# Between two graph layers: four chunks in turn on ScalarE, and the attention weights loaded in that stretch

## The chip, the cores and the metric

The kernel runs on one core of a Trainium2 chip. The metric is the device time of one execution in microseconds (us); lower is better. Times of whole executions are medians of several runs; all times inside the execution come from one profiled execution, counted in us from the start of its span.

## The reference

There are 3125 nodes with 256 features and 50000 edges sorted by target. Two layers follow one another; each adds a graph convolution and an attention to `x`, then a mixture of experts. Around the change, the reference computes:

```python
x = x + L0_ffn(layernorm(x))            # 8 experts, 2 per node: two rows per node come back
xn = layernorm(x)
x = x + L1_gnn(xn, edges) + L1_mix(xn)
# L1_gnn: per node 2 x (64 features, 4 attention scores) = xn @ W; per edge a softmax-weighted
#         sum, over the edges of a target, of the source's row
# L1_mix: q, k, v = xn @ Wqkv.T; dots = k_normed.T @ v_normed; out = q @ dots / n @ Wout.T + bout
```

## The kernel before

`x` stays in SBUF as 125 partitions x 25 tiles x 256, and is worked through in seven chunks of tiles (`CHUNKS`: four of 4 tiles, three of 3).

The **stretch between the layers** is `experts_in` (line 1357). Layer 0's experts have scattered two rows for each node into `y2` in HBM. `experts_in` issues the loads of all seven chunks at once, as tiles `y_in`; the first half of each chunk goes on SyncE's queue (SP), the second half on ScalarE's own queue (ACT). The helper `move` (line 63) splits each load into one DMA of 112 and one of 13 partitions, so there are 14 DMAs on each of the two queues. Then, chunk by chunk:

- `moments` (line 1372): VectorE adds both halves into `x`, takes mean and variance (`bn_stats`, `bn_aggr`), and ScalarE takes the square root.
- `table` (line 1382): VectorE takes the reciprocal and the negative mean (lines 1385 and 1386); ScalarE normalises each tile (`ln_row`, line 1390); TensorE transposes into `ln_pt` (line 1395); ScalarE copies the transposed rows to `xT` (line 1396); TensorE multiplies each tile by `wcat` into a PSUM tile `pw` (line 191), and ScalarE copies each of these 136 columns wide results into `t1_st` (line 1401). SP stores the chunk to the table `tab1` in HBM.

The order is written out by hand for TensorE, VectorE, ScalarE and SP: `moments` of chunk c, then the whole of `table` of chunk c-1. So all of ScalarE's steps for one chunk stand one after another, with TensorE's steps between them.

The **edge loop** follows in `layer1_mix` (lines 1307 to 1332). For 49 groups of 8 edge columns, GpSimd gathers 8 x 128 rows of `tab1` by indirect DMA (`fetch`, line 1212, four buffers `g1`; 391 gathers in all), VectorE makes messages (`messages`, line 1219, line 1223 the first instruction), and TensorE sums them into targets (`products`). A gather can read any row of `tab1`, so the first one waits for the last store. In between, `galerkin` (line 1501) does the attention in steps (`next(todo)`). Before its first `yield` it loads four weight tiles `nat4` to `nat4d` (512 KB each) and `bout` on SP (lines 1512 and 155), transposes three of the tiles into `wkv` and `woT` (lines 1520 to 1528), adds `bout` to all chunks of `x` on VectorE (line 1533) and takes the mean of each head out of `wkv` (lines 1536 to 1538). Only then come the first messages.

The tiles of the loop lie in pools that reuse the memory of `experts_in`; `late` (line 1196, GpSimd), `top` (line 1204) and `dots` (line 1530) are the first instructions to touch it. In the loop and its preparation TensorE, VectorE and ScalarE follow the written order; SP and GpSimd are placed by the framework's planner. Layer 1's expert stage (`layer1_ffn`) begins when the loop and its tail are done.

Of the kernel before, what the change touches and what calls it, by code (L numbers as in the profile page):

```python
# [8 lines left out]
F32 = mybir.dt.float32  # L9
# [9 lines left out]
D = 256  # L19
P = 125  # L20
NT = 25
CHUNKS = ((0, 4), (4, 4), (8, 4), (12, 4), (16, 3), (19, 3), (22, 3))
# [40 lines left out]
def move(queue, out, in_):  # L63


    for s in (slice(0, 112), slice(112, P)):
        queue.dma_start(out[s], in_[s])  # L67
# [7 lines left out]
def rows_of(table):  # L75
    return table.rearrange("(t p) d -> p t d", p=P)
# [12 lines left out]
class Kernel:  # L89
# [1082 lines left out]
    def layer1_mix(self):  # L1172
        nc, tc, a = self.nc, self.tc, self.a
        W, HD = 68, 64
        with ExitStack() as m:
            E_ = mybir.EngineType
            xp = m.enter_context(tc.tile_pool(name="l1x", bufs=1))
            xT = xp.tile([128, 2, N], F32, name="xT2")
            tab1 = self.tab1 = self.dram.tile([N, 2 * W], F32, name="tab1")
            with tc.tile_pool(name="l1l", bufs=1) as lp, \  # L1180
                    tc.tile_pool(name="l1lp", bufs=3, space=PSUM) as pl, \
                    tc.tile_pool(name="l1lm", bufs=4, space=PSUM) as pm, \
                    tc.manual_schedule(engines={E_.PE, E_.DVE, E_.Activation, E_.SP}):
                self.experts_in(lp, pl, pm, xT)
            big = m.enter_context(tc.tile_pool(name="l1", bufs=1))
            wk = m.enter_context(tc.tile_pool(name="l1w", bufs=2))
            gp = m.enter_context(tc.tile_pool(name="l1g", bufs=3))
            ps_a = m.enter_context(tc.tile_pool(name="l1pa", bufs=2, space=PSUM))
            ps_c = m.enter_context(tc.tile_pool(name="l1pc", bufs=1, space=PSUM))
# [22 lines left out]
            def fetch(j0):  # L1212
                n = min(GROUP, NJ - j0)
                g = gp.tile([128, GROUP, 2 * W], F32, name="g1", bufs=4)
                for i in range(n):
                    gather(nc, g[:, i, :], tab1[:], self.t_src[:, j0 + i:j0 + i + 1])
                return j0, n, g
# [61 lines left out]
            def weigh(n, o, v):  # L1279
                nc.vector.tensor_mul(v[:, :n, :, :HD], o[:, :n, None, :HD].to_broadcast([128, n, 4, HD]),  # L1280
                                     v[:, :n, :, HD:].to_broadcast([128, n, 4, HD]))
# [23 lines left out]


            with tc.manual_schedule(engines={E_.PE, E_.DVE, E_.Activation}):
                todo = self.galerkin(big, wk, ps_a, ps_c, xT)
                next(todo)
                starts = [(j0, min(GROUP, NJ - j0)) for j0 in range(0, NJ, GROUP)]  # L1310
                G = len(starts)
                ahead = [fetch(starts[i][0]) for i in range(3)]
                msg, exps, summed = {}, {}, {}
                for i in range(G + 2):
                    if i + 3 < G:
                        ahead.append(fetch(starts[i + 3][0]))
                    if i < G:
                        j0, n, g = ahead[i]
                        o, s, pt = messages(j0, n, g)
                    next(todo, None)  # L1320
                    if 0 <= i - 1 < G:
                        weigh(starts[i - 1][1], msg[i - 1][0], exps[i - 1][2])
                    if i < G:
                        pb = maximum(pt)
                    if 0 <= i - 1 < G:
                        summed[i - 1] = products(*starts[i - 1], exps[i - 1][2], msg[i - 1][1])
                    if 0 <= i - 2 < G:
                        add(*starts[i - 2], *exps[i - 2][:2], summed[i - 2])
                    if i < G:
                        msg[i] = o, ones_of(j0, n)  # L1330
                        exps[i] = exponents(n, s, pb)
                    next(todo, None)
                last = exps[G - 1][0]
# [6 lines left out]
            keep = big.tile([128, 1], F32, name="keep")  # L1340
# [7 lines left out]
            for t0, n in CHUNKS:  # L1348
                s = slice(t0, t0 + n)
                for t in range(t0, t0 + n):  # L1350
                    for h in range(4):
                        xs = self.x[:, t, h * HD:(h + 1) * HD]
# [1 line left out]
                                                       op0=OP.mult, op1=OP.add)  # L1354
        self.layer1_any_order()

    def experts_in(self, pool, psum, psum_m, xT):

        nc, W = self.nc, 68
        mv = pool.tile([P, NT, 2], F32, name="ln_mv2")
        rs = pool.tile([P, 2, NT], F32, name="ln_rs2")
        y2 = self.y2[:2 * N].rearrange("(i t p) d -> p i t d", i=2, p=P)
        loads = []
        for t0, n in CHUNKS:
            r = pool.tile([P, 2, 4, D], F32, name="y_in", bufs=len(CHUNKS))
            for i, queue in enumerate((nc.sync, nc.scalar)):
                move(queue, r[:, i, :n, :], y2[:, i, t0:t0 + n, :])
            loads.append(r)  # L1370

        def moments(r, t0, n):
            s = slice(t0, t0 + n)
            for i in range(2):
                nc.vector.tensor_add(self.x[:, s, :], self.x[:, s, :], r[:, i, :n, :])
            st = pool.tile([P, 4, 6], F32, name="ln_st2", bufs=2)
            for t in range(t0, t0 + n):
                nc.vector.bn_stats(st[:, t - t0, :], self.x[:, t, :])
                nc.vector.bn_aggr(mv[:, t, :], st[:, t - t0, :])
            nc.scalar.activation(rs[:, 0, s], mv[:, s, 1], AF.Sqrt, bias=self.eps[:P])  # L1380

        def table(t0, n):
            s = slice(t0, t0 + n)

            nc.vector.reciprocal(rs[:, 0, s], rs[:, 0, s])
            nc.vector.scalar_tensor_tensor(rs[:, 1, s], mv[:, s, 0], -1.0, rs[:, 0, s], op0=OP.mult, op1=OP.mult)
            row = pool.tile([P, 4, D], F32, name="ln_row2", bufs=2)
            for i in range(n):
                t = t0 + i
                nc.scalar.activation(row[:, i, :], self.x[:, t, :], AF.Identity, bias=rs[:, 1, t:t + 1],  # L1390
                                     scale=rs[:, 0, t:t + 1])
            for k in range(2):
                pt = psum.tile([128, 4, P], F32, name="ln_pt")
                for i in range(n):
                    nc.tensor.transpose(pt[:, i, :], row[:, i, k * 128:(k + 1) * 128], self.ident[:P, :P])
                nc.scalar.copy(xT[:, k, t0 * P:(t0 + n) * P], pt[:, :n, :].rearrange("p a b -> p (a b)"))
            st = pool.tile([P, 4, 2 * W], F32, name="t1_st", bufs=2)
            for i in range(n):
                pm = psum_m.tile([P, 4, 65], F32, name="pw").rearrange("p h c -> p (h c)")[:, :2 * W]
                self.token_matmul(pm, xT, t0 + i, self.wcat)  # L1400
                nc.scalar.copy(st[:, i, :], pm)
            move(nc.sync, rows_of(self.tab1)[:, t0:t0 + n, :], st[:, :n, :])

        before = None
        for r, chunk in zip(loads, CHUNKS):
            moments(r, *chunk)
            if before is not None:
                table(*before)
            before = chunk
        table(*before)  # L1410

    def layer1_any_order(self):

# [84 lines left out]
                nc.vector.tensor_mul(o, o, den[:, :n, :, None].to_broadcast([P, n, 4, HD]))  # L1498
                nc.vector.tensor_add(self.x[:, s, :], self.x[:, s, :], acc[:, :n, 4:])

    def galerkin(self, big, wk, ps_a, ps_c, xT):

        nc, a = self.nc, self.a
        nats = []
        for name, src in (("nat4", a["L1_mix_Wqkv"][512:1024, :].rearrange("(c p) d -> p c d", p=128)),
                          ("nat4b", a["L1_mix_Wqkv"][1024:1536, :].rearrange("(c p) d -> p c d", p=128)),
                          ("nat4c", a["L1_mix_Wout"].rearrange("(c p) f -> p c f", p=128)),
                          ("nat4d", a["L1_mix_Wqkv"][0:512, :].rearrange("(c p) d -> p c d", p=128))):  # L1510
            nat = wk.tile([128, 2, 512] if name == "nat4c" else [128, 4, D], F32, name=name, bufs=1)
            nc.sync.dma_start(nat, src)
            nats.append(nat)
        bout = self.bcast(big, "L1_mix_bout")
        wkv = big.tile([128, 2, 1024], F32, name="wkv")
        for c4 in range(2):
            for k in range(2):
# [10 lines left out]
            nc.scalar.copy(woT[:, :, cc * 128:(cc + 1) * 128], pt)  # L1528
        dots = big.tile([128, 4, 128], F32, name="dots")
        nc.vector.memset(dots, 0.0)  # L1530
        for t0, n in CHUNKS:
            xs = self.x[:, t0:t0 + n, :]
            nc.vector.tensor_add(xs, xs, bout[:, None, :].to_broadcast([P, n, D]))
        heads = wkv.rearrange("p k (h c) -> p (k h) c", c=64)
        mean = big.tile([128, 32], F32, name="wkv_mean")
        nc.vector.tensor_reduce(mean, heads, AX.X, OP.add)
# [40 lines left out]
        for i in range(2):  # L1577
            pm = ps_a.tile([128, 2, D], F32, name="ln_pt")
# [8 lines left out]
        pm = ps_a.tile([128, 2, D], F32, name="ln_pt")  # L1587
# [7 lines left out]
        for t0 in range(0, NT, 2):  # L1595
            m = min(2, NT - t0)
            pm = ps_a.tile([P, 2, D], F32, name="ln_pt")
# [3 lines left out]
            xs = self.x[:, t0:t0 + m, :]  # L1601
# [397 lines left out]
```

## Time and profile before

| what | value |
|---|---|
| median of 3 runs | 3148.76 us (3139.96 to 3158.86) |
| the profiled execution's own time | 2766.24 us |
| its span | 2764.5 us |
| mean granted TensorE clock in it | 0.884 |
| stretch: last instruction of layer 0's experts on GpSimd to first gather | 1535.39 to 1612.23 us |
| first messages of the edge loop | 1634.98 us |
| last gather of the edge loop | 2189.54 us |

The profile tells for every engine what ran when, and for each idle stretch which event ended it. The profiled execution is 382 us shorter than the median of the timed runs, and nothing shown says in which stages those lie.

### The profile page before, as it was taken

How to read it: one execution, taken by the hardware profiler on the slowest of the kernel's cores; microseconds unless marked ns; L12 is line 12 of the kernel's file. 1: busy time of each engine (PE TensorE's matmuls, PEld its weight loads, DVE VectorE, ACT ScalarE, POOL GpSimd, SP SyncE). 2: the span in 40 equal slices, each digit the busy share in tenths (PEclk: the TensorE clock that was granted, in tenths of full speed). 3: DMA queues.
4: the chain of work that ended last, by engine and by line, in shares of the span. 5: the costliest groups of instructions: out<-in, count | busy, mean ns of one | idle time of the engine just before them, and what ended most of it. 6: DMA issues, size and time to landing. Idle time of an engine off the chain costs nothing. (4 is left out here: it accounts for less than half of the span.)

```text
span 2764.5 us, 26618 instructions
## 1 busy us (share of the span) xinstructions
PE 2192.9 (79%) x9047; PEld 1649.0 (60%) x9047; DVE 1502.0 (54%) x3575; ACT 545.3 (20%) x1115; POOL 1660.4 (60%) x1486
## 2 busy tenths in 40 slices
PE   1762659999976997899999459998777756999953
PEld 1541447866754665788888336665655544666643
DVE  7986499455477901122112449998777760222226
ACT  2420000000011111222222234444000021223313
POOL 4888787774000813666666158778777507777751
PEclk9955669999986999999999669999898868999976
DMA  8930534133400303455554421111111121112252
GB/s 296 382 111 14 118 76 107 43 72 91 115 32 2 87 19 130 157 179 180 191 196 139 113 76 47 48 48 45 47 48 49 37 68 39 26 40 60 54 105 71
DMA packets 175937, 259.79 MB, mean 94 GB/s; under 512 B 53839, under 2 KB 140857, under 8 KB 172402
## 3 DMA queue, kind: packets, MB, share of 16 engines
q1 hardware_dynamic: 114273, 198.43, 23.2%
q0 software_dynamic: 52288, 47.17, 7.3%
q10 hardware_dynamic: 9222, 12.30, 1.5%
q8 instruction: 76, 1.25, 0.2%
q14 instruction: 78, 0.64, 0.1%
HBM read 173.99 MB, written 83.69 MB: 93 GB/s over the span
## 5 line engine op out<-in xcount | busy, mean ns | idle before, releaser
L58 POOL DMA_INDIRECT adj<-ch_sum,ch_place x391 | 506.3, 1295 | 150.4 <-issue 111.6
L51 POOL DMA_INDIRECT g<-tab,t_src x391 | 459.6, 1175 | 119.7 <-issue 106.8
L58 POOL DMA_INDIRECT sorted<-s_rows,pos x256 | 245.1, 958 | 183.5 <-DVE s_rows L1059 114.0
L460 PE MATMUL psum<-sup,adjT 125*125 125x256 f32 x1250 | 294.4, 395 | 51.0 <-DMA adjT<-adj 40.3
L1288 PE MATMUL pw<-v,hot 128*125 128x260 f32 x1244 | 306.9, 407 | 0.0
L51 POOL DMA_INDIRECT G<-tabg,g_src x256 | 253.7, 991 | 80.2 <-issue 71.5
L460 PEld LDWEIGHTS psum<-sup,adjT 125*125 125x125 f32 x1250 | 242.1, 195 | 92.9 <-DMA adjT<-adj 42.5
L1288 PEld LDWEIGHTS pw<-v,hot 128*125 128x125 f32 x1244 | 244.4, 200 | 43.6
L866 PE MATMUL ph<-xs,w 128*128 128x256 f32 x960 | 219.1, 387 | 23.1 <-issue 20.1
L866 PEld LDWEIGHTS ph<-xs,w 128*128 128x128 f32 x960 | 183.3, 193 | 58.0 <-issue 33.4
L894 PE MATMUL py<-w,h 128*128 128x256 f32 x960 | 216.7, 379 | 0.0
L1715 PE MATMUL fpy<-fw,fh 128*125 128x256 f32 x800 | 184.9, 387 | 33.6 <-DVE y L1717 28.3
L894 PEld LDWEIGHTS py<-w,h 128*128 128x128 f32 x960 | 180.1, 190 | 23.3
L1715 PEld LDWEIGHTS fpy<-fw,fh 128*125 128x125 f32 x800 | 151.5, 191 | 71.1 <-DVE y L1717 29.9
L868 ACT ACTIVATE h<-ph,b 128x256 f32<-128x256 f32 x240 | 113.7, 474 | 361.1 <-PE ph L866 329.3
L1707 PE MATMUL fph<-xT,fw 128*128 128x500 f32 (+1 forms) x448 | 175.5, 541 | 0.2 <-DMA fw<-in_L_ffn_W_dram 0.2
L1034 PE MATMUL pctx<-s_mv,s_ro 128*128 128x256 f32 x512 | 155.5, 415 | 1.9 <-DVE s_mv L1033 1.9
L58 POOL DMA_INDIRECT slots<-rows,abi x50 | 72.7, 1455 | 100.8 <-DVE r_cum L948 85.8
L897 DVE TENSOR_SCALAR yo<-py,own 128x256 f32<-128x256 f32 x60 | 27.8, 481 | 190.8 <-PE py L894 190.8
L1709 ACT ACTIVATE fh<-fph,cols 128x500 f32<-128x500 f32 (+1 forms) x112 | 70.3, 633 | 295.6 <-PE fph L1707 262.5
L463 DVE TENSOR_TENSOR x<-x,psum 125x512 f32<-125x512 f32 (+1 forms) x104 | 68.7, 663 | 109.6 <-PE psum L460 109.5
L1707 PEld LDWEIGHTS fph<-xT,fw 128*128 128x128 f32 x448 | 84.8, 190 | 71.4 <-issue 48.6
(537 smaller groups left out, 3352.8 us busy)
## 6 DMA issues: line engine op xcount, KB each, us to landing
adjT<-adj SPq DMA_DIRECT2D x25, 1367.2 KB
adj<-zero SPq DMA_DIRECT2D x22, 1536.0 KB
w<-in_L_ffn_W1p_dram SPq DMA_DIRECT2D x30, 1024.0 KB
w<-in_L_ffn_W2p_dram SPq DMA_DIRECT2D x30, 1024.0 KB
slots<-empty SPq DMA_DIRECT2D x1, 8448.0 KB
srow<-slots SPq DMA_DIRECT2D x30, 264.0 KB
adj<-ch_sum,ch_place POOLq DMA_INDIRECT x391
g<-tab,t_src POOLq DMA_INDIRECT x391
```

Source lines behind the costliest of these rows:

```text
L51: nc.gpsimd.indirect_dma_start(out=out, out_offset=None, in_=table, in_offset=bass.IndirectOffsetOnAxis(ap=idx, axis=0))
L58: return nc.gpsimd.indirect_dma_start(out=table, out_offset=bass.IndirectOffsetOnAxis(ap=idx, axis=0), in_=rows, in_offset=None, **kw)
L460: nc.tensor.matmul(pm[:, i, :], mats[b][:, (a0 + i) * P:(a0 + i + 1) * P], sup[:, b, :], start=(b == b0), stop=(b == b0 + n - 1))
L463: nc.vector.tensor_add(xs, xs, pm[:, :m, :])
L866: nc.tensor.matmul(ph, w1[:, k, f * 128:(f + 1) * 128], xs[:, k, :], start=(k == 0), stop=(k == 1))
L868: nc.scalar.activation(h[:, f, :], ph, AF.Gelu, bias=b1[:, f:f + 1])
L894: nc.tensor.matmul(py, h[:, f, i * 128:(i + 1) * 128], w2[:, f, :], start=(f == 0), stop=(f == FC - 1))
L1034: nc.tensor.matmul(p1, ro[:, f - f0, :], mv, **st)
L1288: nc.tensor.matmul(pw.rearrange("p h c -> p (h c)"), hot[:, i - i0, :], v[:, i, :, :].rearrange("p h c -> p (h c)"), start=(i == i0), stop ...
L1707: nc.tensor.matmul(ph[:, :n * P], w1[:, k, f * 128:(f + 1) * 128], xT[:, k, t0 * P:(t0 + n) * P], start=(k == 0), stop=(k == 1))
L1709: nc.scalar.activation(hs[:, f, :n * P], ph[:, :n * P], AF.Gelu, bias=self.col("L1_ffn_b1", ei * FC + f))
L1715: nc.tensor.matmul(py, hs[:, f, i * P:(i + 1) * P], w2[:, f, :], start=(f == 0), stop=(f == FC - 1))
```

## The change

It has three parts.

1. The loads. Both halves of every `y_in` chunk are issued on SP; ScalarE issues none. Behind them on SP, still in `experts_in`, come the four attention weight tiles and `bout` (`attention_weights`). These tiles now live in the pool `l1x` beside `xT`.
2. The order. `table` is cut into `rows` (reciprocal, negative mean and normalising), `turned` (transposes and copies to `xT`) and `table` (multiplication, copies, store). One turn of the loop takes `moments` of chunk c, `rows` of c-1, `turned` of c-2 and `table` of c-3. Two tiles' results share one PSUM tile and are copied by one instruction, so 25 copies become 14; `t1_st` has three buffers, where it had two.
3. The bias. The seven additions of `bout` to `x` stand at the end of `experts_in`, ahead of the edge loop's stage, and no longer in `galerkin`.

```diff
         for t0, n in CHUNKS:
             r = pool.tile([P, 2, 4, D], F32, name="y_in", bufs=len(CHUNKS))
-            for i, queue in enumerate((nc.sync, nc.scalar)):
-                move(queue, r[:, i, :n, :], y2[:, i, t0:t0 + n, :])
+            for i in range(2):
+                move(nc.sync, r[:, i, :n, :], y2[:, i, t0:t0 + n, :])
             loads.append(r)
+        nats, bout = self.attention_weights(keep)
...
-        def table(t0, n):
+        def rows(t0, n):
...
+            return row
+
+        def turned(row, t0, n):
             for k in range(2):
...
                 nc.scalar.copy(xT[:, k, t0 * P:(t0 + n) * P], pt[:, :n, :].rearrange("p a b -> p (a b)"))
-            st = pool.tile([P, 4, 2 * W], F32, name="t1_st", bufs=2)
-            for i in range(n):
-                pm = psum_m.tile([P, 4, 65], F32, name="pw").rearrange("p h c -> p (h c)")[:, :2 * W]
-                self.token_matmul(pm, xT, t0 + i, self.wcat)
-                nc.scalar.copy(st[:, i, :], pm)
+
+        def table(t0, n):
+            st = pool.tile([P, 4, 2 * W], F32, name="t1_st", bufs=3)
+            for i in range(0, n, 2):
+                m = min(2, n - i)
+                pm = psum_m.tile([P, 2, 256], F32, name="pw")[:, :, :2 * W]
+                for j in range(m):
+                    self.token_matmul(pm[:, j, :], xT, t0 + i + j, self.wcat)
+                nc.scalar.copy(st[:, i:i + m, :], pm[:, :m, :])
             move(nc.sync, rows_of(self.tab1)[:, t0:t0 + n, :], st[:, :n, :])
...
-        before = None
-        for r, chunk in zip(loads, CHUNKS):
-            moments(r, *chunk)
-            if before is not None:
-                table(*before)
-            before = chunk
-        table(*before)
+        ready = {}
+        for c in range(len(CHUNKS) + 3):
+            if c < len(CHUNKS):
+                moments(loads[c], *CHUNKS[c])
+            if 0 <= c - 1 < len(CHUNKS):
+                ready[c - 1] = rows(*CHUNKS[c - 1])
+            if 0 <= c - 2 < len(CHUNKS):
+                turned(ready.pop(c - 2), *CHUNKS[c - 2])
+            if 0 <= c - 3 < len(CHUNKS):
+                table(*CHUNKS[c - 3])
+        for t0, n in CHUNKS:
+            xs = self.x[:, t0:t0 + n, :]
+            nc.vector.tensor_add(xs, xs, bout[:, None, :].to_broadcast([P, n, D]))
+        return nats
```

`attention_weights` holds the loads that stood at the head of `galerkin`, unchanged but for the pool:

```diff
+    def attention_weights(self, pool):
...
+            nat = pool.tile([128, 2, 512] if name == "nat4c" else [128, 4, D], F32, name=name, bufs=1)
+            nc.sync.dma_start(nat, src)
+            nats.append(nat)
+        bout = self.bcast(pool, "L1_mix_bout")
+        return nats, bout
```

More of the change, by code (lines that the diff above doesn't have):

```diff
@@ L1183, in layer1_mix @@
                     tc.manual_schedule(engines={E_.PE, E_.DVE, E_.Activation, E_.SP}):
-                self.experts_in(lp, pl, pm, xT)
+                nats = self.experts_in(lp, xp, pl, pm, xT)
             big = m.enter_context(tc.tile_pool(name="l1", bufs=1))
@@ L1307, in layer1_mix @@
             with tc.manual_schedule(engines={E_.PE, E_.DVE, E_.Activation}):
-                todo = self.galerkin(big, wk, ps_a, ps_c, xT)
+                todo = self.galerkin(big, wk, ps_a, ps_c, xT, nats)
                 next(todo)
@@ L1355, in layer1_mix, with experts_in @@
         self.layer1_any_order()
-    def experts_in(self, pool, psum, psum_m, xT):
+    def attention_weights(self, pool):
+        nc, a = self.nc, self.a
+        nats = []
+        for name, src in (("nat4", a["L1_mix_Wqkv"][512:1024, :].rearrange("(c p) d -> p c d", p=128)),
+                          ("nat4b", a["L1_mix_Wqkv"][1024:1536, :].rearrange("(c p) d -> p c d", p=128)),
+                          ("nat4c", a["L1_mix_Wout"].rearrange("(c p) f -> p c f", p=128)),
+                          ("nat4d", a["L1_mix_Wqkv"][0:512, :].rearrange("(c p) d -> p c d", p=128))):
+            nat = pool.tile([128, 2, 512] if name == "nat4c" else [128, 4, D], F32, name=name, bufs=1)
[3 more added lines that the diff above has]
+        return nats, bout
+    def experts_in(self, pool, keep, psum, psum_m, xT):
         nc, W = self.nc, 68
@@ L1499, in layer1_any_order, with galerkin @@
                 nc.vector.tensor_add(self.x[:, s, :], self.x[:, s, :], acc[:, :n, 4:])
-    def galerkin(self, big, wk, ps_a, ps_c, xT):
+    def galerkin(self, big, wk, ps_a, ps_c, xT, nats):
         nc, a = self.nc, self.a
[L1506 to L1514, printed above, removed]
         wkv = big.tile([128, 2, 1024], F32, name="wkv")
@@ L1530, in galerkin @@
         nc.vector.memset(dots, 0.0)
-        for t0, n in CHUNKS:
-            xs = self.x[:, t0:t0 + n, :]
-            nc.vector.tensor_add(xs, xs, bout[:, None, :].to_broadcast([P, n, D]))
         heads = wkv.rearrange("p k (h c) -> p (k h) c", c=64)
```

## The prediction

> **What bounds the kernel now.** The page's first part gives no engine more than 79% of the span, so I read the stretch that is edited and then what follows it. First the waits between 1536 and 1640 us, longest first (engine, line, what it waited for, us, times, longest):
>
> ```profile
> POOL late L1196 <- DMA tab<-t_st: 74.8, 1, 74.8
> ACT L1380 <- DMA y_in<-y: 40.3, 1, 40.3
> ...
> DVE ln_rs L1385 <- ACT ln_rs L1380: 21.6, 5, 9.5
> DVE top L1204 <- DMA tab<-t_st: 12.5, 1, 12.5
> DVE x L1533 <- SPq L1418: 11.3, 1, 11.3
> ```
>
> GpSimd does nothing for 74.8 us, until the last table store lands. VectorE loses 21.6 us to square roots. The "SPq L1418" of the last line had long been done; what that addition still lacked is its load, `bout`. Then ScalarE's and GpSimd's timelines:
>
> ```profile
> 1538.36 24.10 ACTq L67 DMA_DIRECT2D y_in<-y  x14
> 1562.48 1.28 ACT L1380 ACT_TABLE_LOAD   x1 [40.33 <-DMA y_in<-y]
> 1563.78 0.49 ACT L1380 ACTIVATE ln_rs<-ln_mv,eps 125x4 f32<-125x4 f32 x2
> ...
> 1611.16 0.10 POOL L1196 MEMSET late<- 128x1 f32 x1 [74.81 <-DMA tab<-t_st]
> 1612.23 0.98 POOL L51 DMA_INDIRECT g<-tab,t_src  x1 [0.96 <-POOL late L1196]
> ```
>
> ScalarE spends 24.10 us issuing 14 DMAs (each 0.31 us; it is held up between them[...]), and takes the first root at 1563.8, though VectorE had the moments at 1549.97. From 1562.48 to its last copy (1608.54) it is the pace: a chunk of four costs 7.1 us (roots at 1572.08, 1579.16, 1586.26), in which it waits for TensorE (12.7 us in all before the copies of `pw`). Store and landing take it to the first gather, 1612.23.
>
> Who paces the edge loop? In the waits of 1660 to 2190 us, VectorE's and GpSimd's longest:
>
> ```profile
> DVE msg L1223 <- DMA g<-tab,t_src: 66.1, 44, 3.4
> POOL g L51 <- issue: 97.8, 321, 0.3
> POOL g L51 <- DMA g<-tab,t_src: 5.2, 17, 0.3
> ```
>
> In 44 of some 46 groups the messages wait for the gather, and GpSimd waits for nobody (0.3 us of issue between gathers). So GpSimd, gather after gather, carries the end: the loop's end moves with the **first gather**, not with the first messages (1634.98).
>
> **What the Trainium skill says.** *DMA: Bandwidth & Descriptors*, "Issuing engines are not separate DMA queues": DMAs of several engines run on the same 16 DMA engines, and a second issuer saves only issue time. The trace agrees and more: in tenths of a microsecond from 1537, SP alone and then both queues,
>
> ```profile
> GB/s 287 369 246 0 0 0 0 0 0 0 0 0 0 0 0 0 0 0 0 0 0 113 154 82 72 0 0 61 164 184 297 317 358 399 379 369 369 379 399 338
> ```
>
> SP alone reaches 369 to 399 GB/s; with both, 1540 to 1565 has a mean of 240. *SBUF — State Buffer*, "Who interferes with whom": a VectorE instruction with two SBUF inputs contends with a GpSimd one that reads SBUF. The trace agrees: while `bout` is added, four gathers take 1.54, 1.97, 1.70 and 1.43 us, not 0.94. *TensorE: Matmul & The Clock Gate*, "What's actually happening": the clock is halved when idle and released by activity; the granted clock here is 0.50 until 1570 and 0.84 in 1570 to 1575.
>
> **Part by part.** *Loads.* ScalarE loses its 24.1 us of issuing. SP issues 28 loads, then 5. At 370 GB/s the 6.4 MB take 17 us from 1539.1, at 240 they take 27. The first chunk, 1.02 MB, lands near 1543 by the former (2.8 us plus about 1.2 to signal, as now), at 1545.2 as now by the latter. The 2.2 MB of weights follow, another 6 to 9 us: all issued by about 1565 to 1572. Queued behind them on SP are the table stores; the first comes at about 1563 to 1568 and can wait a few us; only the last, 20 us later, is waited for. I take 1543.
>
> *Pace.* With ScalarE free VectorE sets it. Its chunk of four takes 4.92 us (1564.40 to 1569.32), that of three 3.68 plus 0.25 for the two small ones. From 1543.0: `moments` end at 1547.7, 1552.4, 1557.3, 1562.2, 1566.1, 1570.1 and **1574.0**. A landing is late only if its chunk misses these starts; at 240 GB/s none does by over 2.2 us. ScalarE needs per turn a root (0.3), four normalisings (2.06), two copies (1.16) and two of 272 columns. Those the trace does not show: copies of 136, 375 and 500 columns take 0.27, 0.475 and 0.58, so 0.39 by interpolation; *ScalarE: Activation LUTs*, "What ACT_TABLE_LOAD costs", gives 186 ns + 0.833 per element, 0.41. I take 0.39. Sum 4.3 us, under 4.92. TensorE's turn takes about 3.7 us at full clock (8 transposes 1.3, 16 multiplications 2.4), 6.7 at half: if it stays slow it adds up to 2 us a turn. VectorE no longer waits for roots: each is a turn old.
>
> *Tail.* The price of the depth: after 1574.0 ScalarE still has, in order, rows 5 (1.57), turned 4 (0.86), table 3 (0.78), rows 6 (1.57), turned 5 (0.86), table 4 (0.66), turned 6 (0.86), table 5 (0.66), then table 6 behind its multiplications (1.8 us at full clock, 3.0 at half) and 0.66: 10.3 to 11.5 with the multiplications, about 1 more for handovers. Last copy about 1586. Store, landing, `late` and first gather take 3.7 as now (1608.54 to 1612.23): **first gather near 1590, 22 us earlier**.
>
> *Bias.* The seven additions (7.24 us) run from about 1574.5 to 1583, the last after rows 6 has read `x`; cover: ScalarE's tail, to 1586. Uncovered they delay only `wkv`'s mean. Out of the gathers' time they give GpSimd back 0.60 + 1.03 + 0.76 + 0.49 = **2.9 us**, unless other work slides in there; then 0.
>
> *Weights.* On landing by 1572 at the latest they cost nothing: transposes and copies (1614.90 to 1621.98, part of it waiting) become about 5 us from 1587, and the mean (4.8 us) ends by 1600. The first group has 8 gathers at 1.25 plus about 2 to land: 1602. First messages move 33 us, from 1635 to 1602, but 10 of these are no gain in a loop that follows GpSimd.
>
> Larger tiles in `l1x`: 17 KB more per partition. They shift the others; nothing in the trace prices that. Bounds: gain 2 us, loss 5; taken 0.
>
> Sum: 22 + 3 = 25 us of 2766.24, **2741** in the profile. The timed runs are 382 us longer and the trace does not show where. As a lump outside, 25 remains 25 and gives 3124; spread evenly, 25 x 3148.76 / 2766.24 = 28.5. I take the latter: **3120**. About 0.5%, 16 us, is what a measurement of this kernel tells from no change.
>
> **Rivals.** *B: the messages count.* If in timed runs TensorE or VectorE paces the loop (TensorE is 92% busy in 1700 to 1800 us at clock 1.00; a lower clock would fill it), the loop moves with its first messages: 33 us, up to 37 scaled, 3112 to 3116. Against: the 44 waits.
>
> *C: the stretch gives less.* Loads at 150 GB/s bring the last chunk at 1582 and the first gather to 1602; or TensorE at half clock adds 2 us in four turns. Gain 10 to 17 with the bias: 3132 to 3139. For: a single queue with 1 KB rows was seen alone for under 2 us here; against: the weights came at 303 GB/s on SP alone (1612 to 1615).
>
> *D, slower: one queue starves the stretch.* The first gather comes about 20 us after the last landing (3.7 + 12 + 3.7). Even with before, counting the 2.9, means a last landing at 1595: 6.4 MB in 56 us, **114 GB/s**; below that rate it loses. At 85 GB/s, landing 1614 and first gather 1634: 19 us lost, about 3168 to 3170. Against: every rate above.
>
> *E: it doesn't do what it says,* since one queue's stop holds all: no more than C.
>
> **How the numbers follow.** Chances: forecast 0.63 (gain 18 to 34), B 0.12, C and E 0.19, D 0.06. The low end is B with some spread, 3106; the high end most of C, 3137. Faster by over 0.5%: 0.61 + 0.12 + 0.08 = 0.81; within: 0.13, C's smaller gains and 0.02 of spread; slower: 0.06.
>
> **What would show it.** Right: ScalarE's first root near 1549; last `moments` near 1574; first gather 1586 to 1594; first messages 12 us later, not 23; gathers of that time at 0.94 us; 44 waits of the messages as before. Wrong: VectorE waiting for `y_in` in mid stretch (C, D); waits of ScalarE for TensorE in every turn (C); a first gather 20 us earlier, with a last one that is not (the loop's pace is not GpSimd's); another length after the loop.

## The result, and the profile after

| what | before | after |
|---|---|---|
| median of the timed runs | 3148.94 us (14 runs) | 3124.68 us (14 runs) |
| ratio, with its 95% interval | | 0.9919 [0.9896, 0.9941], some 25.5 us less |
| span of the profiled execution | 2764.5 us | 3119.1 us |
| mean granted TensorE clock in it | 0.884 | 0.843 |

The forecast was 3120 (3106 to 3137), faster. Two of the 14 executions before fell in a slower state (3205 and 3209 us) and are left out of the ratio, which is therefore not the quotient of the two medians.

The two profiled executions are of different length, so their spans can't be subtracted. I read both from one mark, the start of the last scatter of `y` by GpSimd (1535.4 before, 1788.0 after), and cut the difference of 354.6 us at the loop's last gather: **+252.6** before the mark, **-24.2** from the mark to the last gather (654.15, now 629.96), **+126.1** behind it. The first and the last part come from the length of the execution and not from the change: three variants of the changed kernel that were profiled in short executions (`e9`, `e10`, `e11`, below) reach the mark at 1529.7 to 1535.1 and need 573.6 to 577.4 us behind the last gather; the kernel before, 1535.4 and 575.0. So the gain is in the edited stretch:

| us after the last scatter of `y` | before | after |
|---|---|---|
| `y_in` loads issued until | 27.1 | 26.3 |
| first and last square root | 28.4, 62.6 | 14.6, 39.1 |
| last copy into `t_st` starts | 72.9 | 47.6 |
| additions of `bout` | 87.7 to 94.0 | 39.7 to 46.0 (starts) |
| **first gather** | **76.8** | **51.5** |
| first messages | 99.6 | 64.3 |
| last gather | 654.1 | 630.0 |
| from first to last gather | 577.3 | 578.4 |

First, the waits of the stretch (1785 to 1900 us; engine, line, what it waited for, us in all, times, longest):

```profile
POOL late L1196 <- SPq L1447: 49.8, 1, 49.8
ACT L1394 <- DMA y_in<-y: 26.5, 1, 26.5
...
DVE x L1389 <- DMA y_in<-y: 8.6, 2, 8.1
...
ACT ln_rs L1394 <- DVE ln_mv L1393: 7.5, 4, 2.9
...
ACT t_st L1422 <- PE pw L191: 0.7, 1, 0.7
```

GpSimd's wait is 25.0 us shorter (it was 74.8; the event named is SP's next one behind the table stores). ScalarE's waits have turned round: it used to be late for VectorE (21.6 us of VectorE's waits for a root), now ScalarE waits for VectorE's moments. Before the copies out of `pw` it waits 0.7 us, where the kernel before had

```profile
ACT t_st L1401 <- PE pw L191: 12.7, 25, 0.9
```

VectorE waits for `y_in` only at the start. ScalarE's timeline (start, us, form, and in brackets the idle time before it) shows the start and the tail:

```profile
1801.29 1.28 ACT L1394 ACT_TABLE_LOAD   x1 [26.50 <-DMA y_in<-y]
1802.59 0.30 ACT L1394 ACTIVATE ln_rs<-ln_mv,eps 125x4 f32<-125x4 f32 x1
1805.74 0.30 ACT L1394 ACTIVATE ln_rs<-ln_mv,eps 125x4 f32<-125x4 f32 x1 [2.86 <-DVE ln_mv L1393]
...
1815.58 0.30 ACT L1394 ACTIVATE ln_rs<-ln_mv,eps 125x4 f32<-125x4 f32 x1 [1.65 <-DVE ln_mv L1393]
...
1818.80 0.67 ACT L1422 COPY t_st<-pw 125x272 f32<-125x272 f32 x2
...
1833.78 0.69 ACT L1422 COPY t_st<-pw 125x272 f32<-125x272 f32 x2
1835.17 0.69 ACT L1422 COPY t_st<-pw 125x272 f32<-125x272 f32 x2 [0.70 <-PE pw L191]
```

The roots come 4.9 us apart (1805.74, 1810.66, 1815.58), VectorE's pace and no longer ScalarE's 7.1, and two 272-column copies, one right behind the other, take 0.67 together. GpSimd's and VectorE's timelines show what follows:

```profile
1838.79 0.10 POOL L1196 MEMSET late<- 128x1 f32 x1 [49.80 <-SPq L1447]
1839.57 0.98 POOL L51 DMA_INDIRECT g<-tab,t_src  x1 [0.68 <-POOL late L1196]
```
```profile
1827.77 7.23 DVE L1438 TENSOR_TENSOR x<-x,b_L_mix_bout 125x1024 f32<-125x1024 f32 x7
...
1852.37 0.72 DVE L1223 TENSOR_TENSOR msg<-g,t_dir 128x544 f32<-128x544 f32 x1 [6.55 <-DMA g<-tab,t_src]
```

The seven additions lie beside ScalarE's tail. The first messages wait for gathers, 12.8 us after the first of them; before, they came 22.8 after it, behind additions and weights. In the loop (1908 to 2438 us) VectorE still waits for the gathers in nearly every group:

```profile
DVE msg L1223 <- DMA g<-tab,t_src: 68.9, 42, 3.4
```

### The profile page after: what moved, and what is told of

It is laid out like the page before. It is cut to its first block, busy times and chain, and to the rows that moved or that the text cites. A ratio compares the mean times of both kernels' runs of the same rounds, so it can differ in the third digit from the quotient of the medians.

```text
span 3119.1 us, 26613 instructions
## 1 busy us (share of the span) xinstructions
PE 2254.7 (72%) x9047; PEld 1666.0 (53%) x9047; DVE 1500.3 (48%) x3575; ACT 541.0 (17%) x1104; POOL 1645.8 (53%) x1486
## 5 line engine op out<-in xcount | busy, mean ns | idle before, releaser
L58 POOL DMA_INDIRECT adj<-ch_sum,ch_place x391 | 490.8, 1255 | 149.4 <-issue 121.8
L51 POOL DMA_INDIRECT g<-tab,t_src x391 | 460.9, 1179 | 119.4 <-issue 116.0
L460 PE MATMUL psum<-sup,adjT 125*125 125x256 f32 x1250 | 325.0, 409 | 225.4 <-issue 167.7
L460 PEld LDWEIGHTS psum<-sup,adjT 125*125 125x125 f32 x1250 | 249.2, 202 | 290.5 <-issue 197.9
L1732 PE MATMUL fpy<-fw,fh 128*125 128x256 f32 x800 | 212.7, 423 | 94.8 <-ACT fh L1726 36.9
L1732 PEld LDWEIGHTS fpy<-fw,fh 128*125 128x125 f32 x800 | 165.9, 211 | 146.7 <-ACT fh L1726 45.0
```

The costliest lines, as they stand in the source:

```text
L51: nc.gpsimd.indirect_dma_start(out=out, out_offset=None, in_=table, in_offset=bass.IndirectOffsetOnAxis(ap=idx, axis=0))
L58: return nc.gpsimd.indirect_dma_start(out=table, out_offset=bass.IndirectOffsetOnAxis(ap=idx, axis=0), in_=rows, in_offset=None, **kw)
L460: nc.tensor.matmul(pm[:, i, :], mats[b][:, (a0 + i) * P:(a0 + i + 1) * P], sup[:, b, :], start=(b == b0), stop=(b == b0 + n - 1))
L1732: nc.tensor.matmul(py, hs[:, f, i * P:(i + 1) * P], w2[:, f, :], start=(f == 0), stop=(f == FC - 1))
```

## The experiments

Two theories. **G** is the forecast's: GpSimd's gathers carry the loop, so time follows the first gather. **M** is rival B: the loop moves with its first messages. Beside these stand the question which part of the change moves the first gather, and the forecast's single steps: the loads' rate, the tail, the bias. Each timed run is set against the kernel before on the same chip; that took 2768 us in one batch (`e9`, `e10`, `e11`) and 3127 to 3149 us in the others. "First gather" is always in us after the last scatter of `y`.

| kernel | ratio to before | in us | first gather | last gather |
|---|---|---|---|---|
| `e1_loads_on_sp` | 0.9972 [0.995, 0.9994] | -9 | 65.8 | 645.7 |
| `e2_order_only` | 0.9971 [0.9954, 0.9987] | -9 | 61.6 | 642.3 |
| `e3_weights_early` | 0.9993 [0.9972, 1.0014] | -2 | 81.9 | 663.0 |
| `e8_two_queues` | 0.9958 [0.9937, 0.9979] | -13 | 61.7 | 637.0 |
| `e4_after_again` | 0.9905 [0.9874, 0.9936] | -30 | 52.1 | 630.2 |
| `e6_weights_late` | 0.9923 [0.9892, 0.9954] | -24 | 51.6 | 629.8 |
| `e7_bias_late` | 0.9933 [0.9915, 0.995] | -21 | 52.2 | 628.1 |
| `e9_extra_gather` | 1.0097 [1.008, 1.0113] | +27 | 52.9 | 687.7 |
| `e10_split_120` | 0.9905 [0.9886, 0.9925] | -26 | 58.6 | 634.2 |
| `e11_pool_adds` | 0.9917 [0.99, 0.9933] | -23 | 51.9 | 628.8 |
| `e12_weigh_scalar` | 1.0042 [1.0026, 1.0059] | +13 | 51.6 | 651.7 |

### Which part: `e1_loads_on_sp`, `e2_order_only`, `e8_two_queues`, `e3_weights_early`

`e1` is the kernel before with both halves of the loads on SP, and nothing else:

```diff
-            for i, queue in enumerate((nc.sync, nc.scalar)):
-                move(queue, r[:, i, :n, :], y2[:, i, t0:t0 + n, :])
+            for i in range(2):
+                move(nc.sync, r[:, i, :n, :], y2[:, i, t0:t0 + n, :])
```

> The kernel before with one edit: both halves of each y_in chunk are issued on SyncE. Theory G (the edge loop follows GpSimd, so the gain is what the first gather gains): ScalarE's first root comes 12 us earlier (about 16 us after the last scatter of y instead of 28), the chunks then keep their pace of 7.1 us, first gather 12 us earlier, 65 us after the last scatter instead of 77; total 12 us shorter (ratio 0.996). Theory M (the first messages count): the same here, 12 us. If one queue alone carried 370 GB/s in the long run, SyncE would have issued all 28 loads in about 17 us; at the two queues' rate in 23 to 25 us.

First gather 11.0 us earlier, and 9 (2 to 16) in the time. The first root comes at 14.5 instead of 28.4, 13.9 earlier. The old order gives 3 of these back: before, the moments of two chunks lay ready when ScalarE came free, and its second root followed after 0.2 us; here the second comes 3.2 after the first. From there each chunk of four costs 7.1 us or more, as before.

`e2` is the changed kernel with ScalarE issuing half of the loads again, and with weights and bias where they were (so the order, two tiles per copy and the third `t_st` buffer together; their shares were not separated):

```diff
-            for i in range(2):
-                move(nc.sync, r[:, i, :n, :], y2[:, i, t0:t0 + n, :])
+            for i, queue in enumerate((nc.sync, nc.scalar)):
+                move(queue, r[:, i, :n, :], y2[:, i, t0:t0 + n, :])
...
-        nats, bout = self.attention_weights(keep)
```

> The kernel before with the new order alone (rows, turned, table in turn, two tiles per copy); loads still on two queues, weights and bias still in galerkin. Theory G: ScalarE starts at 27 us after the last scatter as before, but then VectorE's 4.9 us per chunk is the pace; first gather near 63 us instead of 77, total 12 to 15 us shorter. If TensorE's half clock set the pace (6.7 us per turn), the gather would come only a few us earlier and ScalarE would wait for TensorE in every turn.

First gather 15.2 us earlier, and 9 (4 to 14) in the time. Its ScalarE timeline shows what the order can't mend while the loads are issued there:

```profile
1784.23 23.02 ACTq L67 DMA_DIRECT2D y_in<-y  x14
1807.28 1.28 ACT L1393 ACT_TABLE_LOAD   x1 [39.25 <-DMA y_in<-y]
```

Its first root, at 27.3, is 12.7 us later than in the changed kernel. At the first gather the two parts add up: 11.0 + 15.2 = 26.2, together 25.3. In the time they add up less well: 9 + 9 = 18 against 30 (20 to 40) for the whole change on the same chip (`e4`). The intervals are wide enough for that; besides, the loops of `e1` and `e2` took 2.6 and 3.4 us longer than that of the kernel before (579.9 and 580.7), so that at the last gather 8.4 and 11.8 were left.

`e8` puts only the two queues back into the changed kernel:

```diff
-            for i in range(2):
-                move(nc.sync, r[:, i, :n, :], y2[:, i, t0:t0 + n, :])
+            for i, queue in enumerate((nc.sync, nc.scalar)):
+                move(queue, r[:, i, :n, :], y2[:, i, t0:t0 + n, :])
```

> The changed kernel with the y_in loads on both queues again; order, weights and bias as changed. ScalarE is held until 26 us after the last scatter and starts at 27, VectorE's 4.9 us per chunk from there: first gather at 62 to 64 us instead of 52. Theory G: 10 to 12 us longer than the changed kernel, 13 to 15 us under before. If the loads on one queue gave nothing (the two queues' rate being the same), no difference.

First gather 61.7, as in `e2`: of the 25.3 us, 10.1 hang on ScalarE's issuing alone. The loads themselves went hardly faster with two issuers: all were issued 25.8 us after the mark here and 27.1 in the kernel before, where 28 by SP alone end at 26.3. That fits what the Trainium skill says under "Issuing engines are not separate DMA queues" in *DMA: Bandwidth & Descriptors*: a second issuer saves only the time of issuing. What it cost here is time of ScalarE.

`e3` is the kernel before with weights and bias early (loads after `y_in`, additions at the end of `experts_in`), with its two queues and its order:

```diff
+        nats, bout = self.attention_weights(keep)
...
         table(*before)
+        for t0, n in CHUNKS:
+            xs = self.x[:, t0:t0 + n, :]
+            nc.vector.tensor_add(xs, xs, bout[:, None, :].to_broadcast([P, n, D]))
+        return nats
```

> The kernel before with the third and part of the first edit alone: attention weights and bout loaded behind the y_in loads, bias added at the end of experts_in; order and two load queues as before. The first gather stays at 77 us after the last scatter, the first messages come about 10 us earlier (12.5 us after the first gather, not 22.7). Theory G: 0 us, or up to 3 us shorter if the bias additions out of the gathers' time count. Theory M: 10 us shorter.

In the time no difference that can be told from none (-9 to +4 us), though its first messages come 3.9 us earlier (95.7). The first gather is even 5.0 later, against the expectation, and in this profile the last one 8.9. ScalarE's waits show where 3 of the 5 us arise:

```profile
ACT t_st L1415 <- PE pw L191: 15.7, 25, 0.9
```

It waits 15.7 us for `pw` instead of 12.7, while TensorE's granted clock is 0.58 in the stretch (before: 0.67 in 1535 to 1612). In the old order every copy follows its own multiplications, so slower multiplications would show just there; that the clock is the cause is not shown. I can't say whether the early weights lower the clock or this execution had it by itself.

### Who paces the loop: `e6_weights_late`, `e9_extra_gather`, `e12_weigh_scalar`

`e6` takes the changed kernel and loads the weights and adds the bias in `galerkin` again. The first gather stays, the first messages come late: what G and M disagree on.

```diff
-        nats, bout = self.attention_weights(keep)
...
-        for t0, n in CHUNKS:
-            xs = self.x[:, t0:t0 + n, :]
-            nc.vector.tensor_add(xs, xs, bout[:, None, :].to_broadcast([P, n, D]))
-        return nats
```

> The changed kernel, but weights, bout and the bias additions stay in galerkin as before. First gather as in the changed kernel, 52 us after the last scatter; first messages 22.5 us after it, at 74, not 64. Theory G: as long as the changed kernel, 25 us under before, or up to 3 us longer if the bias additions slow the gathers. Theory M: 10 us longer than the changed kernel, 15 to 25 us under before.

```profile
1847.69 0.72 DVE L1223 TENSOR_TENSOR msg<-g,t_dir 128x544 f32<-128x544 f32 x1
```
```profile
2403.45 1.19 POOL L51 DMA_INDIRECT g<-tab,t_src  x1 [0.30 <-issue]
```

From its mark (1773.61) the first messages start at 74.1 instead of 64.3, 9.7 us later. The last gather comes at 629.8 (changed kernel 630.0), the last messages at 633.1 (633.4). The delay is gone by the loop's end: **G**. The time alone would not decide it, since -24 us has an interval of -34 to -14, and M had forecast -15 to -25. The third part of the change (weights and bias early) brings nothing that these runs can tell: 0.9923 against 0.9919.

What makes the loop as long as it is stands in one line per profile, the gathers' count, busy us, mean ns and the idle time before them. The kernel before, then the changed one:

```profile
L51 POOL DMA_INDIRECT g<-tab,t_src x391 | 459.6, 1175 | 119.7 <-issue 106.8 <-DMA g<-tab,t_src 5.5 <-DVE hot L1272 4.0
L51 POOL DMA_INDIRECT g<-tab,t_src x391 | 460.9, 1179 | 119.4 <-issue 116.0 <-DVE hot L1272 1.5 <-DVE top_b L1252 0.9
```

The idle time is 119.3 to 119.7 us, some 0.30 per gather whatever event is named, in every profile but that of `e12`, early messages or late. GpSimd waits for nobody there, and the loop's length is the gathers' own time.

`e9` gives GpSimd alone more to do, one gather more for each of 49 groups, whose data nothing uses:

```diff
+                more = gp.tile([128, 2 * W], F32, name="g_more", bufs=4)
+                gather(nc, more, tab1[:], self.t_src[:, j0:j0 + 1])
```

> The changed kernel with one more gather in each of the 49 groups of the edge loop, into a tile that nobody reads; a dose of GpSimd's work alone. Theory G (GpSimd's gathers carry the loop): each costs 1.25 to 1.48 us, 61 to 73 us in all, so about 35 to 48 us longer than before (ratio 1.011 to 1.015). Theory M (TensorE or VectorE carries it): VectorE's waits of 1.6 us per group take up the extra gathers for the greater part, and the total stays under before.

The last gather comes some 58 us later than in the changed kernel. The groups of GpSimd and VectorE's wait:

```profile
L51 POOL DMA_INDIRECT g<-tab,t_src x391 | 449.5, 1150 | 119.4 <-issue 113.8 <-DVE hot L1274 2.7 <-POOL late L1196 0.7
...
L51 POOL DMA_INDIRECT g_more<-tab,t_src x49 | 52.7, 1076 | 14.9 <-issue 14.3 <-DMA g_more<-tab,t_src 0.6
```
```profile
DVE msg L1225 <- DMA g<-tab,t_src: 113.9, 40, 15.5
```

The 49 took 52.7 + 14.9 = 67.6 us; the 391 others fell from 460.9 (changed kernel) to 449.5, so net 56. VectorE's wait rose by 45 us in 530 us of the loop (113.9, from 68.9), and by 60 over all of it (141.8, from 82.0): it only waits longer. GpSimd carries the loop's end, gather for gather. In the time it was less than I had expected (+35 to +48), +27 against the kernel before, but M had forecast a time under that kernel's. The changed kernel was not timed in this batch; with its -25.5 from elsewhere the extra gathers cost some 52.

`e12` takes work that holds the gathers off VectorE: in `weigh`, for groups 28 to G-4, 32 ScalarE activations per group replace VectorE's multiplication.

```diff
+                if on_scalar:
+                    for i in range(n):
+                        for h in range(4):
+                            nc.scalar.activation(v[:, i, h, :HD], o[:, i, :HD], AF.Copy,
+                                                 scale=v[:, i, h, HD:HD + 1])
+                    return
```

> A version that may beat both: the changed kernel, where in the second half of the edge loop (groups 28 to 45 of 49) ScalarE, then almost idle, does weigh (line 1280) as 32 scaled copies per group, and VectorE no longer. In the changed kernel one gather per group takes 1.9 us, not 0.94, and it is the one that runs beside weigh, VectorE's 2.3 us long instruction with two SBUF inputs. If GpSimd carries the loop and that instruction holds it up, 18 groups gain 0.95 us each, 17 us: 40 to 45 us under before (ratio 0.986), the loop's gathers 560 us from first to last. If ScalarE's 32 copies (some 0.27 us each, 8.6 us per group of 11.5) come too late for TensorE, the messages no longer wait for gathers and the gain is smaller or turns into a loss of a few us.

```profile
L51 POOL DMA_INDIRECT g<-tab,t_src x391 | 437.8, 1120 | 163.6 <-issue 109.3 <-DVE score L1227 45.8 <-DMA g<-tab,t_src 4.0
```

The gathers did get 23 us quicker (437.8, from 460.9). But the loop got 21.7 longer (600.1), since GpSimd now waits 45.8 us for VectorE, and the last messages start 20.3 us after the last gather, where it was 3.4. That is 38.6 later than in the changed kernel, and the time is some 39 us longer than its (1.0042 to 0.9919), not 15 to 20 shorter. GpSimd no longer sets the pace here. In the windows, columns busy us of PE, PEld, DVE, ACT and POOL, with counts, then PEclk, DMA share and GB/s, this kernel and then the changed one:

```profile
2200.00:2300.00 100.00, 52.76 (x202) 39.99 (x201) 39.63 (x93) 43.95 (x185) 63.72 (x65) 0.73 0.17 45
```
```profile
2200.00:2300.00 100.00, 76.91 (x323) 60.12 (x322) 77.38 (x144) 4.43 (x24) 79.28 (x69) 0.94 0.21 48
```

All of PE, VectorE and GpSimd do less here, so none of them is simply full. VectorE waited for what the profile calls "remote", which the changed kernel's loop has nowhere:

```profile
DVE top L1241 <- remote: 75.7, 5, 19.1
```

I can't tell what that was. So the loss can't be put down to ScalarE's copies coming late, and its cause stays open. What the run does show is that the gathers get quicker when VectorE gives up `weigh`; what else holds the loop when GpSimd does not, it can't say.

### The bias alone: `e7_bias_late`

The changed kernel, with the weights loaded early and only the additions back in `galerkin`:

```diff
-        for t0, n in CHUNKS:
-            xs = self.x[:, t0:t0 + n, :]
-            nc.vector.tensor_add(xs, xs, bout[:, None, :].to_broadcast([P, n, D]))
-        return nats
+        return nats, bout
```

> The changed kernel with the seven bias additions alone put back into galerkin; weights and bout are loaded early. Only the 2.9 us are asked for. If the additions slow the gathers for good, the gathers of the loop take 3 us longer from first to last (581 instead of 578); if other work slides into their place, 578 as in the changed kernel. First messages: the additions (7.2 us) run from about 52 to 60 us and wkv's mean follows to 65, so the messages come at 65 to 66 instead of 64. The total time alone can't tell 3 us.

The gathers beside the additions (GpSimd's timeline) are held, as before:

```profile
1830.42 1.73 POOL L51 DMA_INDIRECT g<-tab,t_src  x1 [0.68 <-POOL late L1196]
...
1832.63 1.77 POOL L51 DMA_INDIRECT g<-tab,t_src  x1 [0.16 <-issue]
1834.70 1.68 POOL L51 DMA_INDIRECT g<-tab,t_src  x1 [0.30 <-issue]
1836.69 1.43 POOL L51 DMA_INDIRECT g<-tab,t_src  x1 [0.30 <-issue]
1838.43 0.94 POOL L51 DMA_INDIRECT g<-tab,t_src  x1 [0.30 <-issue]
```

That is 2.8 us over four times 0.94. The first messages come at 67.8, later than the 65 to 66 expected. Yet the loop, 575.9 from first to last gather, is shorter than the changed kernel's 578.4. Over the profiles whose loop does the same work it is 575.3 to 581.2 with no order by where the bias stands: of the kernels with an early bias, `e8` has the shortest loop and `e3` the longest. A term of 2.9 us is not resolved by these runs.

### The loads' rate: `e10_split_120`, `e11_pool_adds`

In the changed kernel a 125-partition load goes as 112 + 13 partitions (`move`). `e10` splits it 120 + 5:

```diff
-                move(nc.sync, r[:, i, :n, :], y2[:, i, t0:t0 + n, :])
+                for ps in (slice(0, 120), slice(120, P)):
+                    nc.sync.dma_start(r[ps, i, :n, :], y2[ps, i, t0:t0 + n, :])
```

> The changed kernel with the y_in loads split at partition 120 instead of 112 (120 and 5, not 112 and 13). Question: why 28 loads on one queue moved at 240 to 270 GB/s after their first 2 us, where the weights behind them reached 346. If the split of partitions is the cause, the rate rises to 300 or more and SyncE has issued all loads by 20 us after the last scatter, not 26. If the rows' scattered places in HBM or the source are the cause, it stays. Total time: VectorE paces the stretch either way, so the first gather moves by 0 to 2 us; no change of the total that can be measured.

Worse: the first gather comes at 58.6. The last number of a window is GB/s. The changed kernel, 5 to 32 us after the last scatter, and then `e10`:

```profile
1793.00:1795.00 2.00, 0.00 (x0) 0.00 (x0) 0.00 (x0) 0.00 (x0) 0.00 (x0) 0.50 1.08 308
1795.00:1800.00 5.00, 0.00 (x0) 0.00 (x0) 3.54 (x7) 0.00 (x0) 0.00 (x0) 0.50 1.11 264
1800.00:1805.00 5.00, 0.00 (x0) 0.00 (x0) 4.76 (x12) 1.58 (x2) 0.00 (x0) 0.50 1.12 238
...
1820.00:1825.00 5.00, 4.54 (x35) 3.77 (x33) 4.76 (x12) 4.98 (x12) 0.00 (x0) 1.00 1.09 346
```
```profile
1540.00:1545.00 5.00, 0.00 (x0) 0.00 (x0) 3.73 (x10) 0.19 (x1) 0.00 (x0) 0.50 1.05 210
1545.00:1550.00 5.00, 0.00 (x0) 0.00 (x0) 4.02 (x11) 1.39 (x2) 0.00 (x0) 0.50 1.05 201
```

VectorE is at 4.76 of 5.00 with the former, 3.73 to 4.25 until 1560 with the latter: at 200 to 220 GB/s the loads set the pace of the chunks of four, at 240 to 270 VectorE does. So the rate hangs on how the load is cut, but not in the way I had expected, and why this cut gives 240 I didn't settle. (The weights behind the loads come at 346, on 128 partitions, but from another place in HBM and in other tiles, so that is no pure comparison.)

The slower loads explain 3.7 of the 7.0 us by which the first gather is late: the last `moments` end at 42.8, not 39.1. The rest arises in the tail. The table stores stand behind the loads and the weights on SP, where the first of them comes at 37.9, not 31.5, and ScalarE has to wait until a `t_st` buffer has been stored:

```profile
ACT t_st L1423 <- DMA tab<-t_st: 1.8, 1, 1.8
```

One misfit: the timed gain, 26 us (21 to 32), is above the 18.3 by which the first gather and the 20.0 by which the last gather moved. This profile also reaches the mark 5.7 us earlier than that of the kernel before (1529.7, not 1535.4), where the two kernels are the same; so much, at least, two executions can differ there.

`e11` asks whether VectorE's pace is the last one: for all chunks but the first, GpSimd, idle here, adds the two halves.

```diff
-            for i in range(2):
+            if t0 > 0:
+                nc.gpsimd.tensor_add(r[:, 0, :n, :], r[:, 0, :n, :], r[:, 1, :n, :])
+            for i in range(2 if t0 == 0 else 1):
```

> A version that may beat both: the changed kernel, where from the second chunk on GpSimd, idle in this stretch, adds the second half of y_in to the first, and VectorE adds one tile to x, not two. VectorE's chunk of four falls from 4.9 to 3.7 us, ScalarE's 4.3 us become the pace: first gather 3 to 5 us earlier (47 to 49 us after the last scatter), total 3 to 5 us under the changed kernel, too little for the total alone. If the two engines hold each other up (both read two SBUF inputs), or if GpSimd's addition takes more than 4 us, VectorE waits for GpSimd in every chunk and the first gather comes no earlier or later.

No gain, first gather 51.9. GpSimd's first addition, VectorE's next one, and the last square roots and the last copy on ScalarE:

```profile
1549.12 2.34 POOL L1389 TENSOR_TENSOR y_in<-y_in 125x1024 f32<-125x1024 f32 x1 [13.10 <-DMA y_in<-y]
```
```profile
1551.49 1.23 DVE L1391 TENSOR_TENSOR x<-x,y_in 125x1024 f32<-125x1024 f32 x1 [3.31 <-POOL y_in L1389]
```
```profile
1571.62 0.32 ACT L1396 ACTIVATE ln_rs<-ln_mv,eps 125x3 f32<-125x3 f32 x1
...
1574.78 0.34 ACT L1396 ACTIVATE ln_rs<-ln_mv,eps 125x3 f32<-125x3 f32 x1
...
1582.70 0.69 ACT L1424 COPY t_st<-pw 125x272 f32<-125x272 f32 x2 [0.70 <-PE pw L191]
```

At the start GpSimd has to wait for the second chunk to land, and its 2.34 us then stand between the landing and VectorE: the second root comes at 20.0, not 17.7. At the end VectorE is ahead, with its last `moments` done at 37.4, not 39.1, but now ScalarE is late for it: from 1563.85 to its last copy it never waits longer than 0.70, and that copy starts at 48.1, not 47.6. So behind VectorE's pace lie the loads at the start and ScalarE at the end, both close.

### Repeats: `e4_after_again`, `e5_before_again`

Both kernels unchanged, to see how well times and profiles repeat.

> The changed kernel once more, as the measure for the three parts on the same chip: 25 us shorter than before. If the parts add up, e1 and e2 together give about these 25 us under theory G with e3 near 0; under theory M the three would have to give 35.

0.9905 [0.9874, 0.9936], with first gather 52.1 and last 630.2: within 0.6 us of the first profile after.

> The kernel before, unchanged, for a profile in the usual length of execution (3140 us, not 2766) and for the spread of the measure. Both theories: ratio 1.000 within 0.002; first gather 77 us and first messages 99 to 100 us after the last scatter of y, gathers of the edge loop 577 to 581 us from first to last.

1.0001 [0.9982, 1.0021]: the comparison shows no difference where there is none. Only its time is used here.

## Why the prediction was right, point by point

- **GpSimd carries the loop.** Right. The gain, 24.2 us at the last gather and 25.5 (19 to 33) in the time, follows the first gather (25.3), not the first messages (35.3, outside that interval); `e6` delayed the messages by 9.7 with the last gather unmoved, `e9` lengthened the loop by the added gathers.
- **Loads.** The rate was wrong, the consequence right. I took 370 GB/s, from what SP alone had reached in the first microsecond of its loads; now it was 308 for two microseconds and then 238 to 270, about what both queues had carried together. The first addition started at 7.8 after the mark (taken: 7.6), because the first chunk came in the quick part. After that VectorE takes a chunk of 1.02 MB in 4.92 us, which is 208 GB/s, and 238 to 270 are enough for that: the step had this alternative ("none does by over 2.2 us"). `e10`, at 200 to 220, is at the edge, and there VectorE does wait. What I took for proof, 303 GB/s of the weights, was of loads on 128 partitions.
- **Pace.** Right: 4.92 us a chunk, first root at 14.6 (taken: 1549, that is 13.6), last `moments` ending at 39.1 (taken: 38.6). ScalarE's turn stayed under it: it waits for VectorE's moments.
- **Tail.** Mis-sized: 12 us taken, **8.8** measured (1827.11 to 1835.86). The multiplications of the last chunk, taken at 1.8 to 3.0, cost a wait of 0.70, as the rest of them ran beside the copies and TensorE's clock was at 1.00 by then; two copies of 272 columns cost 0.67, not 0.78, since the second starts before the first has ended (a single one takes 0.38 and 0.39 in `e11`, as interpolated); of the 1 us for handovers none is seen. Store to first gather was right: 3.71 (1835.86 to 1839.57), taken 3.7.
- **Bias.** 2.9 us taken; the loop became 1.1 longer instead, and the gathers' busy time went from 459.6 to 460.9. `e7` shows the hold itself (2.8 us), but not its worth, since the loop's length varies by 5.8 us over the profiles. The 2.9 are unconfirmed.
- **Weights.** Right that they cost nothing in the changed kernel (first gather 51.5 with them, 51.6 in `e6` without), and that the first messages come 12 us after the first gather (12.8), not 23.
- **The sum.** 25 forecast in the profile, 24.2 found. That it fits so closely is luck: the tail was taken 3.3 too long, the bias was 4.0 too hopeful, and these two errors cancel. **Scaling** 25 to 28.5 was the step that moved the number off: the profile after is a long execution itself, and in it the loop takes 578.4 us against 577.3 in the short one. The extra length lies before the mark and behind the loop. A lump of 25 gives 3124; measured 3124.7. The timed interval, 19 to 33 us, holds both, so it is the profiles that decide this, not the time. The sign "another length after the loop" did come (701.1 us, not 575.0), but it belongs to the length of the execution: the short profiles of `e9` to `e11` have 573.6 to 577.4.

Rival D needed under 114 GB/s; C needed either 150 GB/s or waits of ScalarE for TensorE in every turn. Neither came, though the rate was nearer to C than I had thought.

## What to carry to other kernels

Find which engine's first instruction the following stage hangs on, and cost a change by how much that one instruction moves; work that starts earlier on a follower is no gain (here 10 of 35 us). Look how long an engine that computes is held by a burst of loads that it issues: here ScalarE was held 24.1 us by 14 issues of 0.31 us each, and to free it of them was worth 10 us. When executions differ in length, cut them at marks and look in which stage the difference lies, before scaling anything.

## What the runs showed that I had not expected

- The holds of the gathers go with VectorE's work, not with the number of gathers. 49 gathers more cost a net 56 to 58 us, some 1.16 each with issue, and the mean of the others fell from 1179 to 1150 ns; when VectorE gave up `weigh` in 18 groups, it fell to 1120. The Trainium skill names the contention (*SBUF — State Buffer*, "Who interferes with whom"); these traces add its size: a gather takes 0.94 us alone, and 1.43 to 1.77 beside the additions of `bout` in `e7`.
- The rate of the `y_in` loads on one queue depends on the cut in partitions: 200 to 220 GB/s with 120 + 5, 238 to 270 with 112 + 13.
- Two kernels with the same layer 0 differ by 250 us ahead of the edited stretch. In 200 to 900 us, the profile after has, as its longest wait,

```profile
DVE x L463 <- remote: 224.3, 8, 41.9
```

and the profile before has no wait for "remote" there. This goes with the execution and not with the kernel: the eight other long profiles read here, of both kernels' variants, have 158 to 199 us of that wait on that line, the three other short ones (`e9`, `e10`, `e11`) none. The timed runs of the kernel before show the same two lengths (2768 us in one batch, 3127 to 3149 in the others). What makes a batch long stays open.
